# First layer of a two-layer metaformer: the output product added to r by GpSimd, from a copy that ScalarE makes

## The chip, the cores and the metric

The kernel runs on one core of a Trainium2 chip. A core has TensorE (PE in the profile, its weight loads are PEld), VectorE (DVE), ScalarE (ACT), GpSimd (POOL) and SyncE (SP), which issues most of the transfers. Each takes its instructions in order and waits on semaphores for the others. The metric is the device time of one execution in microseconds, as the median of several runs.

## The reference

Input is x of 8 images with 128 channels and 64 x 64 positions. There are two layers, each with a mixer and a router with experts. The change touches the mixer of the first layer alone. It runs a selective scan over the 4096 positions in four directions (rows, rows backwards, columns, columns backwards), multiplies each result by an output weight and adds the four. In the scan the state is h = exp(dt A) h + dt x B at each position, with 16 states a channel, and y = h C; dt, B and C are made from xh. What is left out between is a convolution over four positions:

```python
def _mamba(u, in_w, conv_w, conv_b, xproj_w, dt_w, dt_b, A_log, Dp, out_w):
    xz = u @ in_w.T
    xh, z = jnp.split(xz, 2, axis=-1)
    ...
    xh = jax.nn.silu(xc.swapaxes(1, 2) + conv_b)
    ...
    y = _selective_scan(xh, dt, A, Bm, Cm) + xh * Dp
    y = y * jax.nn.silu(z)
    return y @ out_w.T
...
U = jnp.stack([xp, jnp.flip(xp, 1), x_tb, jnp.flip(x_tb, 1)], 0)
Y = jax.vmap(_mamba)(U, ...)
y_fused = gate[0] * y_lr + gate[1] * y_rl + gate[2] * y_tb + gate[3] * y_bt
out = y_fused @ out_w.T
out = skip_gate * out + (1.0 - skip_gate) * skip
```

## The kernel before

The program does the 8 images (batches) one after the other through the first layer, then the experts of the first layer, then the second layer. In the first layer each batch has two stages. The first (`scan_inputs`, L653, interleaved with `route_tokens`, L715, of the batch before) normalises x, writes the projected input to xp (rows) and xt (columns), and puts the skip part into r, a tile of 128 channels by 4096 positions in SBUF. The second (`first_mixer`, L709, which calls `scan_blocks`, L582) runs the scans and adds their outputs to r. `route_tokens` of the same batch then reads r, stores it and routes.

`scan_blocks` splits each of the four directions d into four chunks of 1024 positions, 16 chunks a batch, and each chunk into 16 blocks, 256 blocks a batch. Chunks 0 to 7 are the row directions (d = 0 and 1), chunks 8 to 15 the column directions. A block holds 8 channels with their 16 states on 128 partitions. For one block:

- TensorE makes dA in PSUM, two halves of 512 columns with three bf16 matmuls each (L608); ScalarE takes the exponential of each half in place (L609). The waits are kept for the tile as a whole: the second half's matmuls wait for the first half's exponential. There are two dA buffers.
- GpSimd makes bx = xE * B (L611; three buffers). xE comes by a transfer (L616, four buffers).
- VectorE runs the scan over 1024 positions (L622), multiplies by C into hc (L627), and keeps the last column (L629, the copy of `last`) where the direction goes on. This frees the dA buffer.
- TensorE sums hc over the states into y, for four blocks at a time (L636).

The loop issues dA and bx of block n + 1 in the same turn as the scan of block n. All instructions of an engine keep the order in which the loop writes them (`ordered`, L302).

Around the blocks each chunk has small steps: the table at L565 lists each with the block, counted from the chunk's first, in whose turn it is issued. Negative numbers are preparation for the chunk during the blocks of the chunks before; 12 to 20 are its output, and 16 to 20 fall into the next chunk's first blocks. Within a turn the block's own instructions come first, then the steps of the older chunk, then those of the younger. The steps that matter here:

- `skip` (17): VectorE adds y and D * xs into yt, a tile with one buffer. `gate_y` (18, 19): GpSimd multiplies each half of yt with the gate zs, in place.
- `out_product` (19, 20): TensorE multiplies each half of yt with the output weight into a PSUM bank m. m has two buffers, taken in turn by all small products.
- `out_add` (19, 20): VectorE adds the bank to the place in r. For d = 0 and 1 that is a contiguous or reversed stretch of 512; for d = 2 and 3 it is a transposed view, of which neighbouring elements lie 64 apart.
- In the same turns, for the chunk two further on: `taps` 1 (14 to 18, TensorE), `x_gate` 1 (19, three ScalarE operations that read a bank and end in the tanh gate), `gated` (20, GpSimd), `dt_product` (21, 22), a table load and `relu_abs`, `exp`, `plus_one` (from 21 on, ScalarE), `lost` (23, 24, VectorE, which reads `sp_u`, the result of `plus_one`).

The last two chunks of a batch have no chunk two further on, and after the last block only the remaining steps of chunk 15 run.

Of the kernel before, what the change touches and what calls it, by code (L numbers as in the profile page):

```python
# [12 lines left out]
ALU = mybir.AluOpType  # L13
# [10 lines left out]
S = 512  # L24
# [5 lines left out]
CH = 1024  # L30
# [248 lines left out]
class Net:  # L279
# [154 lines left out]
    def scan_steps(self, ch, xp, r, pl, ps):  # L434
# [4 lines left out]
        nc, d, j = self.nc, ch["d"], ch["j"]  # L439
        pool = nc.gpsimd  # L440
        back = d % 2 == 1
        lo = L - CH * (j + 1) if back else CH * j
        dtb, cb2 = self.w(f"dt_b{d}"), self.cb2[:, d : d + 1]
        start = [lo + (1 - q if back else q) * S for q in range(2)]
        half = [slice(q * S, (q + 1) * S) for q in range(2)]
        ID, TANH = AF.Identity, AF.Tanh
        v = {}
# [4 lines left out]
        def bank(name):  # L452
            p = v[name] = ps.tile([C, S], F32, tag="m", bufs=2, name="m")
            return p
# [94 lines left out]
        def out_product(q):  # L549
            self.mm(bank(f"o{q}"), self.Wo[:, d, :], v["yt"][:, half[q]])  # L550

        def out_add(q):
            p, lo = v[f"o{q}"], CH * j + q * S
            lo = L - S - lo if back else lo
            if d < 2:
                to = r[:, lo : lo + S]
                to = to[:, ::-1] if back else to
            else:
                w0 = lo // 64
                to = r.rearrange("p (h w) -> p w h", w=64)[:, w0 : w0 + S // 64, :]  # L560
                to = to[:, ::-1, ::-1] if back else to
                p = p.rearrange("p (w h) -> p w h", h=64)
            self.tt(to, to, p, ALU.add)

        table = [  # L565
            (-18, taps, 0, (0, 1)), (-17, taps, 0, (2, 3)), (-16, taps, 1, (0,)), (-15, taps, 1, (1,)),
# [8 lines left out]
            (12, z_product, 0), (13, z_product, 1), (13, z_gate, 0), (14, z_gate, 1),  # L575
            (15, gated, v, "zs", 0), (16, gated, v, "zs", 1),
            (17, skip), (18, gate_y, 0), (19, gate_y, 1), (19, out_product, 0), (20, out_product, 1),
            (19, out_add, 0), (20, out_add, 1),
        ]
        return table  # L580

# [1132 lines left out]
```

## Time and profile before

The median of three runs was 21109.04 us (21099.6 to 21120.56). The profiled execution took 21100.1 us, of which the span from first to last instruction is 21098.0 us.

| | whole span | first 11,000 us |
|---|---|---|
| TensorE busy, us | 16896.5 | 8019.8 |
| VectorE busy, us | 15973.0 | 9052.5 |
| ScalarE busy, us | 11555.9 | 6072.5 |
| GpSimd busy, us | 8894.3 | 6898.7 |
| granted TensorE clock | 0.93 | 0.92 |

The eight batches of the first layer take about 1250 us each (the output step of the first batch's first chunk starts at 207.4 us, that of the second batch at 1453.5), of which the 256 blocks take some 1100. The span's slices show it:

```profile
DVE  7979799797988979798354666666666666667886
ACT  6555555555555555555253555555555555555442
POOL 6757577575767757576011111212111121212221
PEclk9989899999999999899687999999999999998999
```

Each digit is the busy share of one of 40 slices of 527 us, in tenths; the fourth row is the TensorE clock that was granted, in tenths. The first 19 slices or so are the first layer's mixer, slices 20 to 22 the experts, the rest the second layer.

In rows of the timeline below, the columns are start and duration in us, engine, line, operation, out<-in, shape, how many instructions are merged in the row, and in brackets the engine's idle time before it with what ended it. In rows of groups the columns after the count are the busy time in us and the mean of one in ns, then the idle time of the engine before them in us with what ended it.

### The profile page before, as it was taken

Reading aid. Unit: us, or ns where it says so; the run is one execution under the profiler, and the core shown is the slowest. Engines: PE = TensorE matmul, PEld = TensorE weight load, DVE = VectorE, ACT = ScalarE, POOL = GpSimd, SP = SyncE. Lnnn points to the kernel's source line nnn. Section 1 sums busy time; section 2 is a strip of 40 time slices with the busy share of each in tenths; the row PEclk is TensorE's granted clock in tenths of the full one; section 3 lists DMA queues with packets and bytes.
Section 4 is the critical chain, followed back from the end, with each engine's and each line's share of the span. In section 5 each row is a group of like instructions: output and inputs, shape, how many; then the busy total and the mean of one; then the engine's idle time right before and its main releaser. Section 6 shows DMA issues by size and latency. Waiting matters only on the chain. (4 is left out here: it accounts for less than half of the span.)

```text
span 21098.0 us, 301814 instructions
## 1 busy us (share of the span) xinstructions
PE 16896.5 (80%) x112733; PEld 8742.5 (41%) x112733; DVE 15973.0 (76%) x21079; ACT 11555.9 (55%) x17646; POOL 8894.3 (42%) x6004
## 2 busy tenths in 40 slices
PE   6777777777777777777887888888888888887999
PEld 2222222222222222222645666666666666664343
DVE  7979799797988979798354666666666666667886
ACT  6555555555555555555253555555555555555442
POOL 6757577575767757576011111212111121212221
PEclk9989899999999999899687999999999999998999
DMA  4434344343444434344441000000000000001110
GB/s 113 130 105 130 101 132 129 104 129 105 130 110 123 129 104 130 103 132 118 137 130 37 25 27 26 25 27 25 27 26 25 26 25 27 25 27 36 40 42 24
DMA packets 804471, 1616.93 MB, mean 77 GB/s; under 512 B 179579, under 2 KB 411931, under 8 KB 802267
## 3 DMA queue, kind: packets, MB, share of 16 engines
q1 hardware_dynamic: 803006, 1597.61, 27.6%
q8 instruction: 893, 14.63, 0.3%
q14 instruction: 572, 4.69, 0.1%
HBM read 1373.56 MB, written 223.74 MB: 76 GB/s over the span
## 5 line engine op out<-in xcount | busy, mean ns | idle before, releaser
L288 PE MATMUL dA<-parts,expand 128*128 128x512 bf16 x12288 | 3445.5, 390 | 2448.5 <-ACT dA L291 1770.3
L330 POOL TENSOR_TENSOR bx<-xE,B 128x1024 f32<-128x1024 f32 x2048 | 4823.0, 2358 | 703.7 <-DVE dA L622 461.9
L291 ACT ACTIVATE dA<-dA,negA 128x512 f32<-128x512 f32 x4096 | 2709.4, 661 | 3726.2 <-PE dA L288 3703.4
L622 DVE TENSOR_TENSOR_SCAN dA<-dA,last,bx 128x1024 f32<-128x1024 f32 x1536 | 3612.6, 2352 | 175.7 <-ACT dA L291 158.5
L288 PEld LDWEIGHTS <-expand 128*128 128x128 bf16 x12288 | 1195.4, 98 | 5231.3 <-issue 4517.6
L291 ACT ACTIVATE E_cm<-ss_p 128x1024 f32<-128x1024 f32 x2048 | 1976.9, 1030 | 1544.2 <-PE ss_p L288 1542.7
L339 DVE SCALAR_TENSOR_TENSOR E_cm<-E_cm,gm_cm 128x1024 f32<-128x1024 f32 x2048 | 2423.9, 1224 | 512.6 <-ACT E_cm L291 511.9
L330 DVE TENSOR_TENSOR hc<-dA,C 128x1024 f32<-128x1024 f32 x2048 | 2508.6, 1225 | 166.7 <-DVE dA L622 3.2
L1131 POOL COPY Sd_cm<-S_cm 64x128 f32<-64x128 f32 x1024 | 800.0, 781 | 2887.0 <-DVE S_cm L330 2754.0
L330 POOL TENSOR_TENSOR xD_cm<-tok_cm,D_cm 128x256 f32<-128x256 f32 x512 | 413.1, 807 | 2915.0 <-PE y_p L288 2795.1
L288 PE MATMUL y_p<-E_cm,pad_cm 128*32 128x128 f32 x32768 | 1389.7, 286 | 18.3 <-DVE E_cm L339 10.1
L288 PE MATMUL ss_p<-ssB_cm,ssA_cm 128*128 128x512 bf16 x4096 | 1242.6, 420 | 188.4 <-ACT E_cm L291 166.9
L622 DVE TENSOR_TENSOR_SCAN dA<-dA,bx 128x1024 f32<-128x1024 f32 x512 | 1174.1, 2293 | 185.4 <-POOL bx L330 130.2
L288 PE MATMUL y<-hc,kt 128*32 128x512 f32 x8192 | 1199.8, 653 | 26.0 <-DVE hc L330 26.0
L288 PEld LDWEIGHTS y_p<-E_cm,pad_cm 128*32 128x32 f32 x32768 | 940.5, 113 | 388.5 <-issue 240.6
L288 PE MATMUL bc_p<-stk_cm,W_cm 128*128 128x256 f32 x4096 | 1019.2, 392 | 23.8 <-DMA stk_cm<-xs 20.8
L330 DVE TENSOR_TENSOR gm_cm<-g_p,kt 128x1024 f32<-128x1024 f32 x512 | 624.3, 1219 | 505.8 <-PE g_p L288 501.0
L339 DVE SCALAR_TENSOR_TENSOR dw<-h,w_second,dw 128x512 f32<-128x512 f32 x1024 | 854.4, 860 | 5.1 <-ACT h L291 1.0
L291 ACT ACTIVATE tok_cm<-tok_p 128x384 f32<-128x384 f32 x1024 | 503.0, 491 | 605.6 <-PE tok_p L288 450.5
L288 PEld LDWEIGHTS bc_p<-stk_cm,W_cm 128*128 128x128 f32 x4096 | 739.9, 190 | 194.7 <-issue 76.8
L291 ACT ACTIVATE BC_cm<-bc_p 128x1024 f32<-128x1024 f32 x512 | 525.0, 1026 | 536.8 <-PE bc_p L288 532.4
L288 PE MATMUL tok_p<-W_cm,stk_cm 128*128 128x200 f32 x4096 | 761.4, 339 | 0.0
(387 smaller groups left out, 30190.7 us busy)
## 6 DMA issues: line engine op xcount, KB each, us to landing
xE<-dtx_d SPq DMA_DIRECT2D x2048, 512.0 KB
dtx_d<-dtx SPq DMA_DIRECT2D x256, 256.0 KB
x<-x SPq DMA_DIRECT2D x192, 256.0 KB
ssA_cm<-cs_cm SPq DMA_DIRECT2D x3072, 4.0 KB
stk_cm<-xs SPq DMA_DIRECT2D x368, 128.0 KB
stk_cm<-y SPq DMA_DIRECT2D x368, 128.0 KB
x<-in_x_dram SPq DMA_DIRECT2D x64, 256.0 KB
x<-r SPq DMA_DIRECT2D x64, 256.0 KB
```

The costliest lines, as they stand in the source:

```text
L288: self.ordered(self.nc.tensor.matmul(out, lhsT=lhsT, rhs=rhs, start=start, stop=stop))
L291: i = self.ordered(self.nc.scalar.activation(out, in_, func, **kw))
L330: self.ordered((eng or self.nc.vector).tensor_tensor(out, a, b, op))
L339: self.ordered(self.nc.vector.scalar_tensor_tensor(out=out, in0=a, scalar=s, in1=b, op0=op0, op1=op1))
L622: self.ordered(nc.vector.tensor_tensor_scan(out=t, data0=t, data1=bx.pop(n), initial=0.0 if ch["j"] == 0 else last[:, q : q + 1], op0=ALU. ...
L1131: nc.gpsimd.tensor_copy(Sd[gr, :, g * hi : (g + 1) * hi], S2[gr])
```

## The change

After each output product ScalarE copies the PSUM bank into the half of yt that the product has just read. The add to r is then made by GpSimd from that copy, two turns later than before. The copies stand at turns 19 and 20, the adds at 21 and 22. The step of VectorE is gone. In the order of ScalarE's instructions the first copy stands behind the exponentials of block 20 and ahead of `x_gate` 1, the second behind the exponentials of block 21 and ahead of those of block 22. On GpSimd the adds stand behind the bx of blocks 22 and 23.

```diff
+        def out_copy(q):
+            self.ordered(nc.scalar.copy(v["yt"][:, half[q]], v[f"o{q}"]))
+
         def out_add(q):
-            p, lo = v[f"o{q}"], CH * j + q * S
+            p, lo = v["yt"][:, half[q]], CH * j + q * S
             lo = L - S - lo if back else lo
...
                 p = p.rearrange("p (w h) -> p w h", h=64)
-            self.tt(to, to, p, ALU.add)
+            self.tt(to, to, p, ALU.add, pool)
...
             (17, skip), (18, gate_y, 0), (19, gate_y, 1), (19, out_product, 0), (20, out_product, 1),
-            (19, out_add, 0), (20, out_add, 1),
+            (19, out_copy, 0), (20, out_copy, 1), (21, out_add, 0), (22, out_add, 1),
```

At the border between two batches the scheduler orders a few instructions anew, because r is now written by another engine: on SyncE's queue the load of the next batch's first tile of x now follows the store of r's first stretch, where it stood ahead of it, and on TensorE the first two means over x stand behind statistics of r.

## The prediction

> **What bounds the kernel now.** I read the 40 slices first: GpSimd (POOL) is above five tenths only in the first half of the span, where the first mixer runs, so everything the change touches lies in the first 10,000 us. Then the groups of that stretch, kept apart by shape.
>
> ```profile
> L330 POOL TENSOR_TENSOR bx<-xE,B 128x1024 f32<-128x1024 f32 x2048 | 4823.0, 2358 | 703.7 <-DVE dA L622 461.9 <-DMA xE<-dtx_d 233.2 <-DVE m L339 3.3
> L330 DVE TENSOR_TENSOR hc<-dA,C 128x1024 f32<-128x1024 f32 x2048 | 2508.6, 1225 | 166.7 <-DVE dA L622 3.2
> L330 POOL TENSOR_TENSOR yt<-yt,zs 128x512 f32<-128x512 f32 x256 | 323.2, 1264 | 104.1 <-DVE yt L339 104.1
> L330 DVE TENSOR_TENSOR r<-r,m 128x512 f32<-128x512 f32 x256 | 248.8, 972 | 119.6 <-PE m L288 119.2
> L540 ACT COPY B<-m 128x512 f32<-128x512 f32 x256 | 150.2, 587 | 124.3 <-PE m L288 124.3
> ```
>
> The fourth row is what is removed from VectorE (DVE): 248.8 us of work and 119.6 us of idling before it. VectorE is busy 947 of the 1035 us of the third batch's blocks (the busy times by window), so it looks like the bound, and 368 us look saved. Averages hide what happens in the blocks where the add stands. So I read the timeline there, counting blocks from the chunk's first: its two output products and adds come at 19 and 20. First a chunk of direction 1 (contiguous add):
>
> ```profile
> 2985.23 1.02 PE L288 MATMUL m<-yt,W_out 128*128 128x512 f32 x2
> 2986.62 0.81 PE L288 MATMUL dA<-parts,expand 128*128 128x512 bf16 x3 [0.37 <-DVE last L342]
> 2988.68 0.81 PE L288 MATMUL dA<-parts,expand 128*128 128x512 bf16 x3 [1.26 <-ACT dA L291]
> 2994.68 1.12 PE L288 MATMUL m<-xs,W_dt 128*128 128x512 f32 x2
> 2995.92 0.81 PE L288 MATMUL dA<-parts,expand 128*128 128x512 bf16 x3
> ...
> 2986.07 0.68 ACT L291 ACTIVATE xs<-m,cb 128x512 f32<-128x512 f32 x1
> 2987.99 0.64 ACT L291 ACTIVATE dA<-dA,negA 128x512 f32<-128x512 f32 x1
> ...
> 2986.48 0.68 DVE L330 TENSOR_TENSOR r<-r,m 128x512 f32<-128x512 f32 x1
> 2991.58 0.69 DVE L330 TENSOR_TENSOR r<-r,m 128x512 f32<-128x512 f32 x1 [0.83 <-PE m L288]
> 3003.64 0.70 DVE L339 SCALAR_TENSOR_TENSOR m<-sp_u,m 128x512 f32<-128x512 f32 x1 [0.53 <-ACT sp_u L291]
> ```
>
> The reader is to see a second chain beside VectorE. TensorE makes half of a dA, ScalarE (ACT) takes its exponential, TensorE makes the other half. At 2988.68 TensorE waited 1.26 us because ScalarE came to the exponential only at 2987.99, held up by the three operations of x_gate from 2986.07 on. From there TensorE runs without a pause through y, the second output product, dA of block 22, y and dt_product (2994.68) to dA of block 23 at 2995.92. And VectorE's `lost` at 3003.64 waits 0.53 us for ScalarE: 7.72 us after that dA. A chunk of direction 2 (transposed add, 1.27 us):
>
> ```profile
> 3409.51 1.13 PE L288 MATMUL m<-xs,W_dt 128*128 128x512 f32 x2
> 3411.26 0.81 PE L288 MATMUL dA<-parts,expand 128*128 128x512 bf16 x3 [0.62 <-DVE hc L330]
> 3420.70 1.44 PE L288 MATMUL dA<-parts,expand 128*128 128x512 bf16 x3 [1.43 <-ACT dA L291]
> ...
> 3406.42 1.27 DVE L330 TENSOR_TENSOR r<-r,m 128x512 f32<-128x512 f32 x1 [0.39 <-PE m L288]
> 3418.98 0.69 DVE L339 SCALAR_TENSOR_TENSOR m<-sp_u,m 128x512 f32<-128x512 f32 x1 [0.65 <-ACT sp_u L291]
> 3424.14 0.70 DVE L339 SCALAR_TENSOR_TENSOR m<-sp_u,m 128x512 f32<-128x512 f32 x1 [0.88 <-ACT sp_u L291]
> ```
>
> Here dA of block 23 waited 0.62 us for VectorE, and `lost` follows again 7.72 us later (3418.98 - 3411.26). So what an edit in blocks 19 to 22 is worth is read at one point: when dA of block 23 starts. The rest of the chunk hangs on it, but for one thing that the third fence shows too: at 3420.70 three dA products take 1.44 us instead of 0.81, TensorE at a lower clock, and the second `lost` waits 0.88 us. In a chunk at full clock (3143.35, 0.81) that wait is 0.25: the low clock costs 0.63.
>
> **The change part by part.** *VectorE, removed:* two adds a chunk (0.69 or 1.27 us each) with the wait before the second. VectorE gets to scans 20 to 22 earlier, but they need exponentials from the other chain, so this pays only where VectorE releases dA of block 23 last: 0.62 us in the direction 2 chunk, 0.28 in direction 1 (TensorE was ready at 2994.68 + 0.96 = 2995.64, the 0.96 being the pitch from a product to the next matmul where nothing is waited for, 2990.42 to 2991.38).
>
> *ScalarE, added:* a copy per product, in program order ahead of block 19's x_gate. Before, x_gate started at 2986.07; the product ends at 2985.23 + 1.02 = 2986.25, and a copy starts some 0.03 after a product's end (B copy at 3429.05, product end 3429.02). Its pitch to the next instruction is 0.49 (C copy at 2617.84, next at 2618.33; 587 ns long). Delay D = 2986.28 + 0.49 - 2986.07 = 0.70 us. Behind the waiting copy stand x_gate and the exponential of block 21, and for that wait TensorE's second half, y, the second product, dA 22, dt_product. The second copy costs nothing: it can start at 2991.54 + 0.70 + 0.03 = 2992.27 and is through by 2992.76, while the next exponential, at 2992.23 before, now comes at 2992.93; 0.17 us of cover is left.
>
> *The sum per chunk:* direction 1: dA 23 at 2995.64 + 0.70 = 2996.34 against 2995.92, **0.42 us later**. Direction 2: 3409.51 + 0.96 + 0.70 = 3411.17 against 3411.26, 0.09 earlier. Read in the same way, the eight contiguous chunks of a batch lose 0.42 (four) or 0.49 (four, where the neighbour chunk is the first or last of a direction), together 3.6; of the transposed ones with such a neighbour (chunks 8 to 13) four gain 0.15 and two 0.09, together 0.8.
>
> *Chunk 14* has no later chunk's x_gate or taps beside it. Its add waited 1.90 us at 3684.85; without it scan 20 starts by its exponential's end, 3683.86, instead of 3686.01, and the chain through the two copies gives scan 23 some 1.8 us earlier: a gain of 1.8.
>
> *The batch's tail* has nothing to cover the new steps. VectorE's last add ended at 3744.33 + 1.24 = 3745.57; now a copy (3744.33 + 0.59) and a GpSimd add of 1.26 end at 3746.2: 0.65 lost. The scheduler also puts the next batch's first x load behind the store of r, which waits for that add, on SP's queue: the load was issued at 3744.36, now near 3746.7. The trace has no such order; bounds are 1 gained (r's statistics go ahead of x's) and 2.4 lost; the r chain is the longer one, so I take the nearer 0.65.
>
> *GpSimd, added:* two adds a chunk, after the bx of blocks 22 and 23 in its queue. Nearest row: 1264 ns (yt<-yt,zs). The transposed, reversed view has no row on GpSimd; its copy to xt, with one strided side, takes 1229, and VectorE paid 1276/689 = 1.85 times, so 1.23 to 2.35; I take 1.27, nearer to GpSimd's own rows. bx of block 24 would be ready at about 2999.6 where scan 24 starts at 3004.65, so the bx behind it are covered; two adds would have to take over 3.8 us each to be felt. At 2.35 only the tail would pay, 2.2 us a batch.
>
> The row first: hc took between 1223 and 1226 ns in all 599 cases of the first 3000 us, though GpSimd was busy two thirds of that time; I see no slowing of one engine by the other. The Trainium skill ("SBUF — State Buffer", section "SBUF: two separate sides") says that VectorE and GpSimd share a port pair under an exclusive lock, taken by any GpSimd operation against a VectorE one with two SBUF inputs. By the rule at its worst each new add would hold VectorE for its whole length, 256 x 1.27 = 325 us more; by the row nothing, and scan and hc each read one operand from PSUM, so I go by the row.
>
> *TensorE's clock.* By that wait (above 0.5 us) 36 of the 48 transposed chunks, but only 19 of the 64 contiguous ones, fell to the low clock around block 24; what sets them apart is TensorE's idle time before dA 23. After the change no chunk has it, so the nearest row is the contiguous rate, 0.3: 22 fewer, 22 x 0.63 = 14 us gained. Bounds: none left, 35 gained; all 112, as TensorE's gap at block 21 grows from 1.26 to 1.96 us, 36 lost.
>
> *Sum:* 3.6 - 0.8 - 1.8 + 0.65 + 0.65 = 2.3 us a batch, times 8 = 18, less 14: **4 us** on the profiled run's 21100.1 (span 21098.0, 2.1 around it): 21104. The median of the runs shown is 21109.0, 9 above; I count half of that gap as spread and half as the level to expect: 21109.
>
> **The rivals.** (a) *VectorE is the bound after all.* For it: 947 of 1035 us. Against it: `lost` waits for ScalarE in every chunk. All 368 us would go: 20,732. A weaker form: the copy costs ScalarE nothing (D = 0). Then chunks gain what VectorE held up, 8 x 0.25 + 6 x 0.83 = 7.0, chunk 14's 1.8, less 1.3: 7.5 a batch, 60 in all, with the clock's 14: 21,031. (b) *Slower: the copy's wait at ScalarE, and the chain behind it.* A batch costs 8 (D - 0.25) + 6 (D - 0.83) - 1.8 + 1.3 = 14 D - 7.5, so with the clock's gain the whole is over 0.2% slower (42 us, about what a measurement can tell from no change) from D = 1.04; without that gain from 0.91. If the copy holds ScalarE for its full 0.59, the product's signal is 0.3 late (D = 1.1) and the longer gap at block 21 takes the clock's gain away: 8 x 7.9 = 63 us, 21,168. For it: D rests on 0.2 us of wait and modelled matmul ends. Against it: 0.03 us from product to copy in the row used. (c) *Slower: GpSimd becomes late.* From 3.8 us an add; at 5 us, 112 chunks x 2.4 = 269 us, 21,370. Against it: the 1264 ns row. (d) *The change doesn't do what it says:* the program's order has 256 copies on ScalarE and 256 adds on GpSimd and none of r<-r,m left, so hardly.
>
> **How the numbers follow.** The forecast (within 42 us of before) 0.61; (a) 0.15, mostly its weak form; (b) 0.19; (c) 0.05. So faster 0.15, same 0.61, slower 0.24. The forecast's own range, D from 0.6 to 0.9 with the clock's gain between none and 35, is 21,075 to 21,150. To leave out no more than 2 in 10 the range takes in (b) and half of the way to (a)'s weak form: 21,050 to 21,170.
>
> **What would show it.** Right: x_gate of block 19 starts about 0.7 us after the exponential before it, with a ScalarE idle before the copy put down to PE m; dA of block 23 waits for nothing from VectorE in all chunks; contiguous and transposed chunks take the same time, about 69.1 us from one yt to the next (now 68.5 to 68.7 and 69.0 to 69.3 at full clock, 0.63 more at the low one); VectorE's busy time falls by 249 us and its idle time grows by about as much; GpSimd's rises by 325. Wrong: idle before bx or scan put down to POOL (c), hc longer than 1226 ns (the lock), chunks of both kinds near 68 us (a) or above 69.6 (b).

## The result, and the profile after

| | before | after |
|---|---|---|
| median, us | 21112.97 (21099.6 to 21120.77, 6 runs) | 21281.8 (21254.77 to 21311.71, 6 runs) |
| profiled execution, us (span) | 21100.1 (21098.0) | 21294.15 (21292.2) |
| VectorE busy, us | 15973.0 | 15772.2 |
| ScalarE busy, us | 11555.9 | 11704.7 |
| GpSimd busy, us | 8894.3 | 9234.2 |
| granted TensorE clock, whole span | 0.928 | 0.920 |

The kernel became slower: 1.0081 times the time before, 95% interval 1.0068 to 1.0094. That is 169 us between the medians and 194 us between the two profiled executions. The forecast was no change.

The span's slices after, as they were shown of before:

```profile
DVE  7878788787887878788354666666666666667887
ACT  6555555555555555555253555555555555555442
POOL 6767677676776757677111111112111112112221
PEclk9989899998999989899687999999999999998999
```

VectorE and GpSimd are moved as the diff says, and only in the first half; ScalarE's 149 us more don't show in its row. At this width the clock's row is nearly the same, so what costs the time isn't to be seen here. The groups of the first 11,200 us, kept apart by shape, are nearer to it (before, the idle time of the scan put down to ScalarE's dA was 158.5 us, and the output products took 292.7 us, 659 ns each):

```profile
L330 POOL TENSOR_TENSOR bx<-xE,B 128x1024 f32<-128x1024 f32 x2048 | 4820.0, 2356 | 439.6 <-DMA xE<-dtx_d 253.6 <-DVE dA L625 176.9 <-DVE m L330 3.6
L625 DVE TENSOR_TENSOR_SCAN dA<-dA,last,bx 128x1024 f32<-128x1024 f32 x1536 | 3615.4, 2354 | 505.5 <-ACT dA L291 475.8 <-POOL bx L330 22.1 <-POOL r L330 5.1
L330 DVE TENSOR_TENSOR hc<-dA,C 128x1024 f32<-128x1024 f32 x2048 | 2508.9, 1225 | 168.6 <-DVE dA L625 4.6 <-PE dA L288 0.9
L330 POOL TENSOR_TENSOR r<-r,yt 128x512 f32<-128x512 f32 x256 | 371.8, 1453 | 17.8 <-ACT yt L553 17.0
L288 PE MATMUL m<-yt,W_out 128*128 128x512 f32 x512 | 371.3, 819 | 22.2 <-POOL yt L330 22.2
L553 ACT COPY yt<-m 128x512 f32<-128x512 f32 x256 | 149.9, 586 | 381.5 <-PE m L288 366.4
```

Three readings. GpSimd isn't late: the scans of the second row waited 22 us for bx, and the 512 scans that start a direction, a group of their own, 134 us; before, these were 16 and 130. And hc has kept its 1225 ns. The scans of the second row wait 317 us more for ScalarE's exponentials. And the fifth row has the cause: the output product itself has become longer, 819 ns instead of 659, and ScalarE's copy waits 366 us for it. Nothing in the product was changed.

The timeline shows where. First a chunk that went as the prediction had it (its `skip` starts at 2753.01; the first two rows are the halves of dA of block 21, then the second output product, dA of block 22 and dA of block 23; then ScalarE):

```profile
2761.52 0.81 PE L288 MATMUL dA<-parts,expand 128*128 128x512 bf16 x3 [0.36 <-DVE last L342]
2764.30 0.81 PE L288 MATMUL dA<-parts,expand 128*128 128x512 bf16 x3 [1.97 <-ACT dA L291]
...
2766.04 1.12 PE L288 MATMUL m<-yt,W_out 128*128 128x512 f32 x2
2767.00 0.81 PE L288 MATMUL dA<-parts,expand 128*128 128x512 bf16 x3
...
2771.26 0.81 PE L288 MATMUL dA<-parts,expand 128*128 128x512 bf16 x3
...
2761.20 0.58 ACT L553 COPY yt<-m 128x512 f32<-128x512 f32 x1
2761.68 0.69 ACT L291 ACTIVATE xs<-m,cb 128x512 f32<-128x512 f32 x1
```

The same places of the next chunk (`skip` at 2822.15), with the second copy and the scan of block 22 below:

```profile
2830.67 0.81 PE L288 MATMUL dA<-parts,expand 128*128 128x512 bf16 x3 [0.37 <-DVE last L342]
2833.45 0.81 PE L288 MATMUL dA<-parts,expand 128*128 128x512 bf16 x3 [1.97 <-ACT dA L291]
2834.18 1.45 PE L288 MATMUL y<-hc,kt 128*32 128x512 f32 x8
2835.57 2.08 PE L288 MATMUL m<-yt,W_out 128*128 128x512 f32 x2
2837.43 1.17 PE L288 MATMUL dA<-parts,expand 128*128 128x512 bf16 x3
...
2842.05 0.81 PE L288 MATMUL dA<-parts,expand 128*128 128x512 bf16 x3
...
2837.68 0.58 ACT L553 COPY yt<-m 128x512 f32<-128x512 f32 x1 [2.67 <-PE m L288]
...
2841.02 2.36 DVE L625 TENSOR_TENSOR_SCAN dA<-dA,last,bx 128x1024 f32<-128x1024 f32 x1 [2.23 <-ACT dA L291]
```

Up to the second row the two are alike to 0.01 us, the gap of 1.97 us included. Then y, the product and the next dA take longer, and dA of block 23 comes 19.90 us after `skip` instead of 18.25: 1.65 us late. The windows of this chunk say why (start and end, length, then busy time and count of TensorE, its weight loads, VectorE, ScalarE and GpSimd; after these the granted clock, the DMA share and GB/s):

```profile
2831.50:2833.50 2.00, 0.06 (x1) 0.05 (x1) 1.97 (x2) 1.86 (x4) 0.58 (x1) 1.00 0.51 121
2833.50:2835.50 2.00, 2.00 (x11) 0.29 (x10) 1.09 (x3) 0.66 (x1) 2.00 (x2) 0.81 0.51 117
2835.50:2837.50 2.00, 2.00 (x7) 0.72 (x4) 1.97 (x1) 0.00 (x0) 2.00 (x2) 0.50 0.54 129
2837.50:2839.50 2.00, 1.25 (x5) 0.43 (x4) 1.29 (x2) 1.25 (x2) 2.00 (x2) 0.84 0.48 117
...
2834.50:2835.00 0.50, 0.50 (x8) 0.00 (x0) 0.00 (x0) 0.50 (x1) 0.50 (x1) 0.73 0.60 147
2838.00:2838.50 0.50, 0.50 (x3) 0.11 (x2) 0.50 (x1) 0.26 (x1) 0.50 (x1) 0.85 0.52 107
```

After a stretch in which TensorE did next to nothing the granted clock falls to one half, and it comes back some 3.4 us later. The last two rows, of half a microsecond each, give the edges: 0.73 is half speed for 0.27 us of the stretch, so from 2834.73 on, and 0.85 is half speed for 0.15 us, up to 2838.15. In the undisturbed chunk it stays at 1.00 throughout.

Why does one chunk lose the clock and the other not, with the same gap? In the clock's records of this execution all 321 falls of the first 11,000 us lie at whole multiples of 3.413 us from each other, to within 0.04 us; 2763.05 and 2834.73 are two places of that grid. Cut there, the two chunks differ:

```profile
2759.63:2763.05 3.42, 2.34 (x8) 0.86 (x7) 3.31 (x4) 2.48 (x5) 3.11 (x2) 1.00 0.50 125
2763.05:2766.46 3.41, 2.16 (x12) 0.65 (x12) 2.64 (x4) 1.86 (x3) 3.19 (x2) 1.00 0.52 130
2831.32:2834.73 3.41, 1.44 (x12) 0.35 (x10) 2.85 (x3) 2.42 (x5) 1.81 (x2) 1.00 0.52 125
```

In the first chunk the grid splits the gap, and TensorE is busy 2.34 and 2.16 us of the two windows. In the second the whole gap lies in one window, TensorE is busy 1.44 us of it, and the clock falls at its end.

Counted over the 112 chunks that have a later chunk's preparation beside them (14 in each batch): the second output product is slow, above 1.3 us, in 85 of them, and was in 1 before. Those 85 take 71.57 us on the mean, the other 27 take 69.33; before, all took 69.28. So 85 x (71.57 - 69.33) = 190 us of the 194 lie here. Two smaller terms nearly cancel: chunk 14 takes 60.31 us instead of 64.18, and from the `skip` of chunk 15 to that of the next batch's first chunk it is 219.00 instead of 214.79; together 0.3 us a batch.

### The profile page after: what moved, and what is told of

Its sections match the earlier page's. It is cut to its first block, busy times and chain, and to the rows that moved or that the text cites. A ratio compares the mean times of both kernels' runs of the same rounds, so it can differ in the third digit from the quotient of the medians.

```text
span 21292.2 us, 301931 instructions
## 1 busy us (share of the span) xinstructions
PE 17062.3 (80%) x112733; PEld 8791.1 (41%) x112733; DVE 15772.2 (74%) x20823; ACT 11704.7 (55%) x17902; POOL 9234.2 (43%) x6260
## 5 line engine op out<-in xcount | busy, mean ns | idle before, releaser
L330 DVE TENSOR_TENSOR hc<-dA,C 128x1024 f32<-128x1024 f32 x2048 | 2508.9, 1225 | 168.6 <-DVE dA L625 4.6
L288 PE MATMUL y<-hc,kt 128*32 128x512 f32 x8192 | 1260.6, 685 | 25.4 <-DVE hc L330 25.4
```

The lines of the kernel that those rows point to most:

```text
L288: self.ordered(self.nc.tensor.matmul(out, lhsT=lhsT, rhs=rhs, start=start, stop=stop))
L330: self.ordered((eng or self.nc.vector).tensor_tensor(out, a, b, op))
```

## The experiments

Three theories. Theory 1: the copy holds up ScalarE, TensorE's gap at block 21 grows from 1.26 to 1.97 us, and after a gap of that length the clock falls where the output product stands. Theory 2: the adds on GpSimd disturb VectorE or the bx behind them. Theory 3: ScalarE's wait by itself, 0.7 us a chunk, is worth more than the prediction reckoned. No edit below changes what the kernel returns. "Slow products" are out of 112 chunks, in the profiled execution; the gap is the most frequent one.

| kernel | gap at block 21, us | slow products | mean of the 112 chunks, us | time, us | against before (95%) |
|---|---|---|---|---|---|
| before | 1.26 | 1 | 69.28 | 21112.97 | |
| after | 1.97 | 85 | 71.03 | 21281.8 | 1.0081 (1.0068 to 1.0094) |
| e1_fill3 | 1.32 | 0 | 69.59 | 21134.8 | 1.0009 (1.0 to 1.0019) |
| e8_fill2 | 1.54 | 5 | 69.72 | 21156.91, one execution | |
| e7_fill1 | 1.76 | 27 | 69.81 | 21154.77, one execution | |
| e3_copy_only | 1.97 | 82 | 71.70 | 21380.63 | 1.0126 (1.0111 to 1.0141) |
| e4_pool_only | 1.26 | 0 | 69.34 | 21118.11 | 1.0003 (0.9994 to 1.0013) |
| e2_late | 1.26 | 0 | 68.67 | 21018.92 | 0.9954 (0.9939 to 0.9969) |
| e5_late_tail | 1.26 | 0 | 68.58 | 20996.09 | 0.9948 (0.9934 to 0.9963) |
| e6_late_dve | 1.26 | 0 | 70.59 | 21271.91 | 1.0077 (1.006 to 1.0094) |

The runs of before beside e1 to e4 had a median of 21113.15, those beside e5 to e8 of 21108.42.

**e1_fill3: after, with the first half of block 21's dA made twice.** ScalarE still waits, GpSimd still adds; only TensorE's gap is filled.

```diff
-                    for i in range(3):
...
+                    for _ in range(2 if u % NQ == 5 and h == 0 else 1):
+                        for i in range(3):
...
```

> The changed kernel, in which TensorE computes the first half of dA of the block after the first output product twice (three matmuls more, the same values), so that it idles some 1.3 us instead of 2.0 before the second half; nothing else. Theory 1 (the longer gap drops TensorE's clock just before the second output product): that product takes 1.1 us again instead of 2.1 in all but a few of the 112 inner chunks (slow in 85 after the change, in 1 before), chunks take 69.0 to 69.2 us instead of 71.0, in all 21,100 to 21,150 us. Theory 2 (the adds on GpSimd disturb the blocks) and theory 3 (ScalarE's wait alone, of 0.7 us a chunk, is worth more than reckoned): no change, 21,260 to 21,300.

Measured 21134.8 us (21115 to 21144, 10 runs), inside theory 1's range. The timeline of the chunk that begins at 2783.64:

```profile
2792.15 1.46 PE L288 MATMUL dA<-parts,expand 128*128 128x512 bf16 x6 [0.37 <-DVE last L342]
2794.93 0.81 PE L288 MATMUL dA<-parts,expand 128*128 128x512 bf16 x3 [1.32 <-ACT dA L291]
...
2796.66 1.12 PE L288 MATMUL m<-yt,W_out 128*128 128x512 f32 x2
...
2801.88 0.81 PE L288 MATMUL dA<-parts,expand 128*128 128x512 bf16 x3
```

The second half of dA comes 11.29 us after `skip` (2794.93 - 2783.64), as in after, where it was 2764.30 - 2753.01. So ScalarE is as late as before the fill, and the product stays at 1.12 us all the same: theory 3 falls, and theory 2 with it. Work that is thrown away gives back 147 of the 169 us. No slow product is left in 112. The chunks take 69.59 us, above the 69.0 to 69.2 expected; a low clock around block 24 (the sum y there longer than 1.5 us) stays in 74 of them, where before had 63.

**e7_fill1 and e8_fill2: after, with one or two throwaway matmuls in the gap** (k below is 1 and 2).

```diff
+                    for i in range(k if u % NQ == 5 and h == 0 else 0):
+                        self.mm(dA[u][:, sg], sel, ch["parts"][:, i, sg], start=i == 0, stop=i == k - 1)
                     for i in range(3):
```

> The changed kernel with one matmul more (the first of dA's first half, a value that is overwritten) in the block after the first output product: TensorE's gap is 1.75 us, between 1.97 (slow product in 85 of 112 chunks) and 1.32 (in none). If the clock falls by a share of idle time in a window, fewer slow products, some 20 to 70; 21,140 to 21,250. If there is a sharp bound below 1.75, as many as after the change, 21,260 to 21,300.

> The same with two matmuls more, a gap of 1.54 us: by a share of idle time 0 to 30 slow products, 21,110 to 21,170; by a sharp bound below 1.5 us as after the change, 21,260 to 21,300.

Slow products by the length of the gap: 1.97 us 85, 1.76 us 27, 1.54 us 5, 1.32 us 0. The share falls step by step with the gap, as expected of a rule on how busy TensorE is over a stretch of time, and against a limit on one pause. The two times don't differ, though 27 and 5 slow products do (22 x 2.24 = 49 us by after's price). In e8 the clock fell more often at block 24 instead, in 73 of its chunks against 40. The two can be priced apart in e7: the 46 chunks with neither take 69.19 us on the mean, the 39 with the low clock at block 24 alone 69.76, the 26 with the slow product alone 70.90. So a slow product costs 1.71 us and a low clock at block 24 0.57, together about after's 2.24. By these prices e7 pays 69 us and e8 50, much closer than the slow products alone would have it.

**e3_copy_only: before, with ScalarE's two copies added and VectorE's adds kept.** The copies go to the half of yt that nobody reads again.

```diff
-            (19, out_add, 0), (20, out_add, 1),
+            (19, out_copy, 0), (20, out_copy, 1), (19, out_add, 0), (20, out_add, 1),
```

> The kernel before with the two copies by ScalarE alone added, at the places that they have in the changed kernel; VectorE still adds from PSUM, and nothing reads the copies. Theory 1: the second output product is slow in some 85 of 112 chunks, 21,270 to 21,330. Theory 2: GpSimd has no adds, so only 0.3 to 0.7 us a chunk, 21,120 to 21,190.

Measured 21380.63 us (21367 to 21386, 4 runs): the loss is there without any add on GpSimd, but it is 50 us beyond the expected range. The timeline of a chunk (`skip` at 2773.10):

```profile
2784.39 0.81 PE L288 MATMUL dA<-parts,expand 128*128 128x512 bf16 x3 [1.97 <-ACT dA L291]
2785.12 1.85 PE L288 MATMUL y<-hc,kt 128*32 128x512 f32 x8
2786.90 2.00 PE L288 MATMUL m<-yt,W_out 128*128 128x512 f32 x2
...
2788.93 0.59 ACT L553 COPY yt<-m 128x512 f32<-128x512 f32 x1 [2.98 <-PE m L288]
...
2789.55 0.69 DVE L330 TENSOR_TENSOR r<-r,m 128x512 f32<-128x512 f32 x1 [3.37 <-ACT yt L553]
```

The gap and the slow product are those of after. But VectorE's add starts 0.03 us after the copy has ended (2789.52), so in this kernel the copy also stands ahead of the add, and VectorE sits idle 3.37 us ahead of block 21's scan. The groups have 398.0 us of such idling. This kernel therefore shows that copies alone bring the slow products (82 of 112), and its time is not a measure of them.

**e4_pool_only: before, with two adds of 128x512 on GpSimd in turns 21 and 22,** on the dead halves of yt. VectorE's adds stay.

```diff
+        def pool_add(q):
+            p = v["yt"][:, half[q]]
+            self.tt(p, p, ch["xs"][:, half[q]], ALU.add, pool)
...
-            (19, out_add, 0), (20, out_add, 1),
+            (19, out_add, 0), (20, out_add, 1), (21, pool_add, 0), (22, pool_add, 1),
```

> The kernel before with two more contiguous adds of 128x512 on GpSimd in each chunk, at the places of the new ones (they add xs to halves of yt that nothing reads any more); no copy, and VectorE adds from PSUM as before. Theory 1: nothing waits for GpSimd there, 21,095 to 21,140. Theory 2: most of the loss, 21,220 to 21,290.

Measured 21118.11 us (21101 to 21143, 10 runs), a ratio of 1.0003: no change. The groups of this kernel:

```profile
L330 DVE TENSOR_TENSOR hc<-dA,C 128x1024 f32<-128x1024 f32 x2048 | 2508.8, 1225 | 166.7 <-DVE dA L626 3.2
L330 POOL TENSOR_TENSOR yt<-yt,xs 128x512 f32<-128x512 f32 x256 | 325.0, 1270 | 10.2 <-PE m L288 10.1
```

325 us of additional GpSimd work, at the same turns, cost the chunks nothing (69.34 us against 69.28), and hc kept its 1225 ns. Theory 2 falls. These adds are contiguous in every chunk; the longer transposed ones of after (up to 1694 ns) weren't tried by themselves. Only the border of two batches is longer: from the `skip` of chunk 15 to the first `pooled` of the next stage 105.1 to 106.4 us, against 102.5 to 102.8 before.

**e2_late: after, with every new step one turn later.**

```diff
-            (19, out_copy, 0), (20, out_copy, 1), (21, out_add, 0), (22, out_add, 1),
+            (20, out_copy, 0), (21, out_copy, 1), (22, out_add, 0), (23, out_add, 1),
```

> The changed kernel with copies and adds one turn later (copies at 20 and 21, adds at 22 and 23), so that the first copy stands behind x_gate and behind the exponentials of block 21. Theory 1: x_gate starts at once again, TensorE's gap is 1.3 us, the clock holds, and what VectorE no longer does is gained: chunks of 68.0 to 68.4 us, 21,040 to 21,080 in all. Theory 2: the adds are as many as before, 21,260 to 21,300. Theory 3: the wait at ScalarE is gone too, as theory 1.

Measured 21018.92 us (21001 to 21025, 4 runs): faster than both kernels, and 21 us better than the lower end expected. The timeline (`skip` at 2757.66):

```profile
2768.25 0.81 PE L288 MATMUL dA<-parts,expand 128*128 128x512 bf16 x3 [1.26 <-ACT dA L291]
...
2775.20 0.81 PE L288 MATMUL dA<-parts,expand 128*128 128x512 bf16 x3
...
2765.64 0.68 ACT L291 ACTIVATE xs<-m,cb 128x512 f32<-128x512 f32 x1
...
2769.74 0.59 ACT L553 COPY yt<-m 128x512 f32<-128x512 f32 x1
```

x_gate starts 7.98 us after `skip`, where it stood before the change, the gap is back at 1.26, and the copy lies behind the exponential of block 21's second half, where ScalarE waits for TensorE anyway. dA of block 23 comes at 17.54. The chunks take 68.67 us, more than the 68.0 to 68.4 expected, so the surplus over the expected time doesn't come from them. Chunk 14 takes 59.30 us instead of 64.18. Of the 99 us between the profiled executions 79 lie up to the `skip` of the last chunk; the rest lies behind the mixer, where the times of all ten kernels spread over 25 us.

Part of the chunks' gain is the clock around block 24: y runs there above 1.5 us in 27 chunks, against 63 before and 87 after. That is in part luck, as far as the traces tell. The chunks that keep the clock take about 68.5 us, nearly 20 windows of the grid (68.27 us), so the grid lies in each chunk nearly as in the one before, and a place that spares the clock is kept for up to ten chunks. In e1, where these chunks take 69.20 us, it wanders, and 74 chunks have the low clock. No run changes the chunk's length alone.

**e5_late_tail: e2, but the last chunk of a batch adds as before,** on VectorE from PSUM and without copies, since nothing covers the new steps there.

```diff
+        last = d == 3 and j == NCH - 1
...
-            self.tt(to, to, p, ALU.add, pool)
+            self.tt(to, to, p, ALU.add, nc.vector if last else pool)
```

> The late kernel, in which the last chunk of each batch is as before the change (VectorE adds from PSUM, no copy), so that the order at the border of two batches is that of the kernel before. If the 4 us that each border costs (last skip to the pooled result 106 to 107 us, 102.6 before) come from the new steps and the new order there: 102.6 again, 25 to 32 us less than the late kernel, 20,985 to 20,995. If the border is slower for another reason (GpSimd's queue): no change, 21,010 to 21,025.

Measured 20996.09 us (20985 to 21016, 4 runs), the fastest of all: 0.9948 of the time before, interval 0.9934 to 0.9963. From the `skip` of chunk 15 to the first `pooled` of the next stage it is 102.7 to 104.0 us, against 106.0 to 107.2 in e2. The gain over e2 is 23 us, where 25 to 32 were expected, and the time lies 1 us above the expected range. The intervals of the two overlap, so the runs don't separate them.

**e6_late_dve: e2, but VectorE makes the adds, from the copy in SBUF.** It asks whether the gain of e2 needs GpSimd at all.

```diff
-            self.tt(to, to, p, ALU.add, pool)
+            self.tt(to, to, p, ALU.add)
```

> The late kernel with the adds on VectorE, from the same copies and at the same turns (22, 23). If the late kernel is faster because VectorE lets go of dA of block 23 earlier, this keeps the part of that gain which comes from the place of the add, but VectorE does its 249 us of adds later in the chunk, where it sets the pace: 21,060 to 21,130. If only the earlier reading out of PSUM by ScalarE matters, as fast as the late kernel, 21,010 to 21,030. With two operands in SBUF the add may also hold up GpSimd: above 21,130.

Measured 21271.91 us, 1.2% slower than e2 and in the last of the three ranges, but it is mostly the add that is held up, and seldom GpSimd. The group of the add, and two of its instructions beside GpSimd's:

```profile
L330 DVE TENSOR_TENSOR r<-r,yt 128x512 f32<-128x512 f32 x256 | 479.2, 1872 | 33.8 <-ACT yt L553 33.8
...
2769.10 1.73 DVE L330 TENSOR_TENSOR r<-r,yt 128x512 f32<-128x512 f32 x1
...
2767.94 2.35 POOL L330 TENSOR_TENSOR bx<-xE,B 128x1024 f32<-128x1024 f32 x1 [0.68 <-DVE dA L625]
...
9615.19 0.68 DVE L330 TENSOR_TENSOR r<-r,yt 128x512 f32<-128x512 f32 x1
9615.21 2.87 POOL L330 TENSOR_TENSOR bx<-xE,B 128x1024 f32<-128x1024 f32 x1 [1.81 <-DMA xE<-dtx_d]
```

From PSUM the same add took 972 ns on the mean. Here it takes 1872, from 680 to 3109. The first add starts while a bx runs and ends 0.54 us after it has ended (2770.83 against 2770.29): it stood still nearly until then, and that bx isn't slowed. The second add starts 0.02 us ahead of a bx: it keeps its 0.68 us, and the bx takes 2.87 instead of 2.35. The Trainium skill ("SBUF — State Buffer", section "SBUF: two separate sides") says that a VectorE operation with two SBUF inputs and a GpSimd operation that reads SBUF exclude each other for a whole instruction; these rows agree.

The waiting is not all of the loss: around block 24 the low clock comes in 105 of the 112 chunks, against 27 in e2. No run separates the two.

## Why the prediction was wrong

**What held.** The copy's wait at ScalarE, D, was put at 0.70 us: x_gate starts 8.67 us after `skip` (2761.68 - 2753.01) instead of 7.97. Chunks that the clock spares take 69.14 or 68.95 us most often (69.33 on the mean), and 69.1 was the forecast for both kinds. The second copy is covered where the product isn't slow: in the spared chunk the exponential behind it waits for nothing. dA of block 23 waits for nothing from VectorE in any of the 112 chunks. GpSimd isn't late and hc isn't longer. Of the rivals, (c) is out, as the scans wait 156 us for bx where they waited 146 before, and so is (d), as 256 copies and 256 adds are there; (a) is out for this version, as chunks that the clock spares are not near its 68 us.

**The step that failed: "TensorE's clock".** It had 14 us gained, and the bound on the other side was 36 lost, "as TensorE's gap at block 21 grows from 1.26 to 1.96 us". The gap was right to 0.01 us. It cost 190 us. Three things were wrong in that step:

- *The place.* Only the known low clock around block 24 was priced. With a gap of 1.97 us the clock falls at the gap itself, in the middle of the chain that the prediction had found to set the chunk.
- *The price.* 0.63 us per chunk came from a place where three bf16 products were slowed. At block 21 y, an f32 product and dA are slowed together, 1.65 us (1.71 in e7), and all 85 of these chunks have the low clock around block 24 too, which gives 2.24 us a chunk.
- *The sign.* TensorE's idle time ahead of dA of block 23 was taken for what makes the clock fall, since the transposed chunks had both. The change took that idle time away, and the low clock around block 24 became more frequent, 87 chunks instead of 63: the 85 whose clock had already fallen at block 21, and 2 of the other 27. With the same idle time gone it came in 74 chunks of e1 and in 27 of e2, so that wait alone doesn't decide it. The correlation over two kinds of chunk was read as a cause. It was also weaker than read: by the length of y 27 of the 64 contiguous chunks had the low clock before, not 19.

e1 shows that the gap is the cause: filled, the loss goes but for 22 us, while everything else of the change stays. e3 shows that the copies alone bring it.

**Rival (b)** had the mechanism in one clause, that "the longer gap at block 21 takes the clock's gain away", but only as the loss of a gain, at 21,168; and it asked for D = 1.1, which wasn't so.

**Terms that were mis-sized, with little effect.** Chunk 14 gained 3.9 us, not 1.8. The batch's border lost 4.2, not 1.3. The transposed add takes up to 1694 ns on GpSimd; 1.27 us was taken, and the bounds were 1.23 and 2.35. At the border nothing covers the adds of the last chunk, which is transposed; e5, which takes the new steps out of that chunk, brings the border down by some 3 us a batch. But e4 has a border nearly as long with adds that don't touch r, so neither the copy nor the order of the loads need be the reason; it stays open.

**The weak form of (a)**, the copy at no cost to ScalarE, was put at 21,031 us. It is a fair account of e2 (21018.92), where the copy stands one turn later.

**The lock.** The rule at its worst was put at 325 us, and the row was chosen over it. For this change that was right: VectorE's scan and hc each read one operand from PSUM. (The Trainium skill, in the section cited there, limits the lock to GpSimd operations that read SBUF, which all of these do.) Had VectorE kept the add and read it from SBUF, the rule would have mattered: the adds of e6 took 256 x (1872 - 972) = 230 us more than before, and e6 lost 253 us against e2. That loss also holds the adds' own time on VectorE and the more frequent low clock.

## What to carry to other kernels

A pause of TensorE that lies on a chain of small matmuls costs more than its own length as soon as it lets the clock fall, so when an edit lengthens a pause, price the work right behind it at half speed, and ask in how many repetitions the pause can fall into one window of the clock's grid. A few throwaway matmuls in the pause are a cheap test of whether the clock is the cause. And an instruction that has to wait for a product should stand where its engine is waiting for that chain anyway: one turn later turned a loss of 0.81% into a gain of 0.46%.

## What the runs showed of the hardware that was not expected

- The clock fell after pauses shorter than 2 us inside running work: with a gap of 1.97 us in 85 of 112 chunks, 1.76 in 27, 1.54 in 5, 1.32 in none. In the chunk shown it then stayed at one half for 3.41 us.
- What decided was how long TensorE was busy in one window of the 3.413 us grid. The first layer's mixer in the ten traces has 25,183 such windows that began at full clock. All 859 in which TensorE was busy less than 0.40 of the time were followed by a fall, none of the 22,405 with 0.50 or more were, and of the 1,919 between 757 were; the two outcomes balance near 0.45. (The ends of matmuls are modelled in a trace, so these shares are rough.) An estimate from this: with the grid laid at every place over the undisturbed chunks and 0.445 taken as the bound, the clock falls at block 21 in a share of 0.58, 0.21, 0.09 and 0 of the places, for the four gaps; the runs had 0.76, 0.24, 0.04 and 0. After has more than its share because its slow chunks take 71.57 us, nearly 21 windows (71.68 us), so the next chunk meets the grid at nearly the same place.
- The Trainium skill ("TensorE: Matmul & The Clock Gate", section "Part 1: The HAM clock gate (the "warmup" mystery)") gives a free-running window of about 3.4 us and half speed after an idle one. The length and the free running agree with the falls of after. But here the window need not be idle: in the one before the fall at 2834.73 TensorE was busy 1.44 us.
- VectorE's add with two operands in SBUF took 680 to 3109 ns beside GpSimd (e6), against 676 to 1277 from PSUM before. The one that started second paid: 222 of the 256 adds began while a bx ran, and took 2010 ns on the mean; 10 began just ahead of a bx and took 682 ns at most, and 9 of those bx took 2513 to 2870 ns, where no bx before took over 2390.
